# Layer 0 of a two-layer transformer: sums, norms, turns and table entries queued behind the additions out of banks

## The chip, the cores and the metric

The kernel runs on one core of one Trainium2 chip. The metric is the device time of one execution in microseconds (us), the median of three runs. The engines are PE (TensorE: matmuls; PEld is its weight load), DVE (VectorE), ACT (ScalarE), POOL (GpSimd) and SP (SyncE, which here issues most DMAs). Each engine works through its own queue in the order written into the program.

## The reference

The input x has 8 batches of 512 tokens with 512 features. Two layers follow each other, and each is attention, then a feed-forward part, with a residual and a layer norm behind both:

```python
x = layernorm(x + L0_attention(x))   # 16 heads of 32, causal, biases on q, k, v, o
x = layernorm(x + L0_experts(x))     # router picks 2 of 8 experts per token; LoRA on router and experts
x = layernorm(x + L1_attention(x))   # 8 query heads of 64, 2 key/value heads, RMS norm first
x = layernorm(x + L1_ffn(x))         # gate/up/down with integer weights, hidden 1408
```

The change concerns L0 attention, the layer norm behind it, and the router's tables, which are made beside it. In L0 attention `softmax(q k^T / sqrt(32))` is taken without a maximum: exponentials `p`, their row sums, and a division at the end.

## The kernel before, in words

`attention0` holds layer 0's attention for all 8 batches. A batch `b` has 4 groups `g` of 4 heads, and a group has 3 units `u` of key tiles (`UNITS`: key tile 0; key tiles 1 and 3; key tile 2, all causal). So a batch has 12 slots `(g, u)`, written (0,0) to (3,2). In each slot:

- `scores` writes the scores of the unit to four banks (`sc`); ACT takes the exponential (`p`, L1618); POOL cuts the triangle above the diagonal (L1628).
- the thunks of `todo[g, u]` run, then `product` of the unit before (`av`, L1657, and the sum of `p` over key tiles into `total`, L1665 on DVE), then the thunks of `late[g, u]`, and in slots with u = 1 `normalise` of the group before: `ones x total` on PE (`rs`, L1672), an inverse on ACT and DVE (`inverse`, L80 and L81), and `aoT = av * inverse` (L1679).

`plan(b)` fills `todo` and `late` with the work beside the scores: the projections of the batch before (`project`, `ps_o`, added to x at L1532), its layer norm (`env.layernorm`: statistics L217 and L218, the power on POOL at L219 and L220, the norm L222, and a DMA of each tile to `router.rows`), its turn, its router logits (`score`), and the queries, keys and values of the next batch.

Queries and keys of two groups (`queries_and_keys`, a "pair") and the values (`values`) are made by seven products instead of eight, on sums of weight blocks (`seven_of_weights`, L812) and of blocks of xT (`seven_of_rows`, L825). Product n is `ps_{n}of7`; `ORDER` is 1, 6, 2, 5, 3, 7, 4. Product 1 goes out of its bank through ACT (L1502, L1519), the others are added to what is there by DVE: `add` (L1472), product 3 of a pair by L1506; product 7 takes two additions. All these results, `ps_o`, `rs`, the logits and the tables go to two PSUM banks in turn (`Banks`, called `mm`): PE can't begin a result until the one two places before it has been taken out.

The turn of the normed batch for the router is made by DVE in blocks of 32 x 32 (`Turn.blocks`, L125) and through memory: four DMAs out (`turns.out`, L130), one back (`turns.back`, L133), for batches 0 to 5; batches 6 and 7 are turned by PE (`turn`). `load_x(b + 1)` (L1395) is issued behind the return by `behind_return`. `choose` and `dispatch` pick experts on DVE two batches later, `one_hot` (L619, L620) makes 16 one-hot rows on DVE, and `enter` sums them on PE into `ps_table` and adds them to the table (L629 to L631).

The order on PE is the order of the program (`in_order(tc)`). The order on DVE, ACT, POOL and SP is made by the framework's scheduler when the program is built: from its own estimates it takes, of the instructions that are ready, the one that the program has first. `tc.issue_after(ins)` ties every instruction in its block that goes to the engine of `ins` behind `ins` in that order; it adds no wait of its own.

In batch 0 the plan also holds the whole of the queries, keys and values of batch 0 (`query`, `key`, `value`), the sums of weights and `out_of_bias`, which takes the value bias through the output weights (`spread`, L1540, `ps_bias`). In the last batch there is no next batch to prepare. Its slots hold the first rows for the experts (`first_rows`, `first_turned`, `begin`) and the loads of the experts' weights (`experts.load`, L845), which go to the room of the attention weights.

Of the kernel before, what the change touches and what calls it, by code (L numbers as in the profile page):

```python
# [800 lines left out]
def seven_of_weights(nc, w, s, by_rows):  # L801

    def block(i, j):
        if by_rows:
            return w.rearrange("p (g i) f -> p g i f", i=2)[:, :, i, 256 * j : 256 * (j + 1)]
        return w[:, 2 * j : 2 * (j + 1), 256 * i : 256 * (i + 1)]

    def sums():
        for out, a, b, op in ((s[:, 0], block(1, 0), block(1, 1), ALU.add), (s[:, 1], s[:, 0], block(0, 0), ALU.subtract),
                              (s[:, 2], block(0, 1), s[:, 1], ALU.subtract),  # L810
                              (block(1, 0), block(0, 0), block(1, 0), ALU.subtract)):
            nc.vector.tensor_tensor(out, a, b, op)  # L812

    return {1: block(0, 0), 2: block(0, 1), 6: s[:, 1], 5: s[:, 0], 7: block(1, 0), 3: s[:, 2], 4: block(1, 1)}, sums


def seven_of_rows(nc, xT, t):

    def block(i, j):
        return xT[:, 2 * i : 2 * (i + 1), 256 * j : 256 * (j + 1)]  # L820

    def sums():
        for out, a, b in ((t[:, 0], block(0, 1), block(0, 0)), (t[:, 1], block(1, 1), t[:, 0]),
                          (block(0, 1), block(1, 1), block(0, 1)), (t[:, 2], block(1, 0), t[:, 1])):
            nc.vector.tensor_tensor(out, a, b, ALU.subtract)  # L825

    return {1: block(0, 0), 2: block(1, 0), 6: t[:, 1], 5: t[:, 0], 7: block(0, 1), 3: block(1, 1), 4: t[:, 2]}, sums
# [525 lines left out]
def attention0(env, guard, keep, routes, experts, dram, banks, tiles_ctx):  # L1353
# [9 lines left out]
    with ExitStack() as phase:  # L1363
# [61 lines left out]
        ones = own.tile([P, HD], F32, name="ones")  # L1425
        nc.gpsimd.memset(ones, 1.0)

        heads, pairs = {}, {}
        aoTs = {}
        mm = banks  # L1430

# [37 lines left out]
            return ps  # L1469

        def add(out, ps, a):
            nc.vector.tensor_tensor(out, ps, a, ALU.add)  # L1472

        def share(n, ps, block):
            if n == 6:
# [13 lines left out]
        def queries_and_keys(b, pair, n):  # L1489
            if n == 1:  # L1490
                pair_of_heads(b, pair)
            room = pairs[b, pair]
            g = 2 * pair
            ps = seven(n, lambda s, n, k: ((q_of, k_of)[s][n][:, pair, ts(k, P)], x_of[n][:, k, :]))

            def block(i, j):
                return room[:, :, i, 256 * j : 256 * (j + 1)]

            if n == 1:
                for s, at in enumerate((V_BQ, V_BK)):  # L1500
                    for i in (1, 0):
                        nc.scalar.activation(block(i, 0)[:, s, :], ps[:, s, :], AF.Identity,  # L1502
                                             bias=vec[:, at + g + i : at + g + i + 1])
            elif n == 3:
                for s in range(2):
                    nc.vector.scalar_tensor_tensor(block(0, 1)[:, s, :], ps[:, s, :], steps[:, s, pair : pair + 1],  # L1506
                                                   block(1, 1)[:, s, :], ALU.add, ALU.add)
            else:
                share(n, ps, block)
# [18 lines left out]
        def project(b, t, out_of_heads=False):  # L1528
            ps = mm([P, D], "ps_o")
            for c in range(ND):  # L1530
                (wide if out_of_heads else multiply)(ps, aoTs[b][:, c, ts(t, P)], wo[:, c, :], c)
            nc.vector.tensor_tensor(xs[b][:, t, :], ps, xs[b][:, t, :], ALU.add)  # L1532
            if t == NT - 1:
                env.layernorm(b, lambda t: router.rows[router.row_at(b, t) :][:P])

        def out_of_bias():
            ps = mm([P, D], "ps_bias")
            for c in range(ND):
                spread = own.tile([P, P], F32, tag="spread", name="spread", bufs=2)
                nc.vector.tensor_scalar(spread, env.ident, 0.0, bias_v[:, c : c + 1], ALU.mult, ALU.add)  # L1540
                multiply(ps, spread, wo[:, c, :], c)
            nc.vector.tensor_tensor(row[:, 1, :], ps, row[:, 1, :], ALU.add)

        x1Ts, logits = {}, {}
# [8 lines left out]
        def room(b):  # L1553
            x1Ts[b] = work.tile([P, ND, S], F32, tag="x1T", name="x1T")

        def blocks(b):
            room(b)
            flat = x1Ts[b].rearrange("p k s -> p (k s)")
            for t in range(NT):
                turns.blocks(flat, t, xs[b][:, t, :])  # L1560
            turns.out(flat)
            returned[0] = turns.back(flat)

        def turn(b, c, mm=mm):
            if c == 0:
# [81 lines left out]
        def product(b, g, u, p, acc):  # L1647
# [14 lines left out]
            for kt in UNITS[u]:  # L1662
                w = S - P * kt
                if u:
                    nc.vector.tensor_tensor(total[:, :, P * kt :], total[:, :, P * kt :], p[:, :, at : at + w], ALU.add)  # L1665
                at += w

        def normalise(b, g, acc):
# [23 lines left out]
        def plan(b):  # L1692
# [4 lines left out]
            if b == 0:  # L1697
                for slot, thunks in {
                    (0, 0): [lambda: value(0, 0), lambda: value(0, 1)],
                    (0, 1): [lambda: value(0, 3), lambda: query(0, 1)],  # L1700
                    (0, 2): [lambda: value(0, 2), lambda: key(0, 1), lambda: pair_of_heads(0, 1)],
                    (1, 0): [lambda: router.merge_lora(mm([P, ND, E], "ps_wr")), lambda: query(0, 2), lambda: key(0, 2), x_sums],
                    (1, 1): [lambda: query(0, 3), v_sums],
                    (1, 2): [lambda: key(0, 3), q_sums, out_of_bias],
                    (2, 0): [k_sums],
                }.items():
                    todo[slot] += thunks
            if b:
                for t, slot in enumerate(((1, 0), (1, 0), (1, 1), (1, 1)) if last else ((1, 0), (1, 1), (1, 2), (2, 0))):
                    todo[slot].append(lambda t=t: project(pb, t))  # L1710
                for n, (to, *slot) in zip(ORDER, ((todo, 0, 0), (late, 0, 0), (todo, 0, 1), (late, 0, 1), (todo, 0, 2), (late, 0, 2), (todo, 1, 0))):
                    to[tuple(slot)].insert(0, lambda n=n: queries_and_keys(b, 1, n))
            if not last:
                if b:
                    todo[2, 0].append(x_sums)
                for n, (to, *slot) in zip(ORDER, ((todo, 2, 0), (todo, 2, 1), (late, 2, 1), (todo, 2, 2), (late, 2, 2), (todo, 3, 0), (late, 3, 0))):
                    to[tuple(slot)].append(lambda n=n: queries_and_keys(b + 1, 0, n))
                for n, (to, *slot) in zip(ORDER, ((todo, 3, 0), (todo, 3, 1), (todo, 3, 1), (late, 3, 1), (todo, 3, 2), (late, 3, 2), (late, 3, 2))):
# [1 line left out]
            if b > 1:  # L1720
                todo[0, 0].append(lambda: choose(b - 2, mm=aside))
                late[0, 2].append(lambda: dispatch(b - 2))
                todo[1, 2].append(lambda: behind(enter(one_hot(b - 2, range(NT))), normed[0]) if last else enter(one_hot(b - 2, range(NT))))
                if last:
                    todo[1, 2].append(soon)
            if b:
                if by_dma:
                    todo[2, 1].append(lambda: blocks(pb))
                    late[3, 2].append(lambda: score(pb))
                else:  # L1730
                    for c in range(ND):
# [32 lines left out]
        for b in range(NB):  # L1764
            todo, late = plan(b)
            for g in range(ND):
                if b and g == 1 and b + 1 < NB:
                    load_xT(b + 1)
                if g == 3 and b + 1 < NB:
                    with behind_return():  # L1770
                        load_x(b + 1)
                if b == NB // 2 and g == 0:
                    experts.load_lora(work, 1)
                if b == NB - 1:
                    for e in ((0,), (), (1, 2), (3, 4, 7))[g]:
                        experts.load(e)
                acc = []
                for u in range(len(UNITS)):
# [701 lines left out]
```

## Time and profile before

| | us |
|---|---|
| median of 3 runs | 2138.12 (2136.28 to 2138.49) |
| profiled execution, its own time | 2130.51 |
| span of its instructions | 2128.7 |
| PE busy in the span | 2049.1 (96%) |
| DVE busy | 1314.0 (62%) |
| ACT busy | 638.9 (30%) |
| POOL busy | 517.3 (24%) |
| mean granted TensorE clock | 0.996 |

Layer 0's attention takes the first 716 us; from 130 us on a batch takes 83 to 86 us. The experts follow, then layer 1. In rows of the timeline the columns are start and length in us, engine, line, operation, output and inputs by the program's names, shapes and count, and in brackets the idle time before the row and what ended it. `experts` as an operand in layer 0 is the room that the attention weights, xT and the values share with the experts' weights. In rows of waits: who waited for whom, total us, times, longest. A wait is put down to the instruction that came last.

### The profile page before, as it was taken

How to read it: one execution, taken by the hardware profiler on the slowest of the kernel's cores; microseconds unless marked ns; L12 is line 12 of the kernel's file. 1: busy time of each engine (PE TensorE's matmuls, PEld its weight loads, DVE VectorE, ACT ScalarE, POOL GpSimd, SP SyncE). 2: the span in 40 equal slices, each digit the busy share in tenths (PEclk: the TensorE clock that was granted, in tenths of full speed). 3: DMA queues.
4: the chain of work that ended last, by engine and by line, in shares of the span. 5: the costliest groups of instructions: out<-in, count | busy, mean ns of one | idle time of the engine just before them, and what ended most of it. 6: DMA issues, size and time to landing. Idle time of an engine off the chain costs nothing. (4 is left out here: it accounts for less than half of the span.)

```text
span 2128.7 us, 40459 instructions
## 1 busy us (share of the span) xinstructions
PE 2049.1 (96%) x17122; PEld 1117.1 (52%) x17122; DVE 1314.0 (62%) x2155; ACT 638.9 (30%) x930; POOL 517.3 (24%) x509
## 2 busy tenths in 40 slices
PE   8888999999997999999999999999999999999998
PEld 2334444444443677775433333333334888888886
DVE  4657876877867733224236888888857644555443
ACT  2334334343443211111133333333332232222222
POOL 1343534444443311132033312322201000000000
PEclk9999999999999999999999999999999999999999
DMA  6014425235154467887631322232201311111000
GB/s 204 2 57 124 141 80 144 88 103 155 61 176 169 169 169 222 248 243 214 188 113 51 114 75 72 98 119 75 65 1 47 102 60 60 60 60 60 20 20 22
DMA packets 193071, 226.29 MB, mean 106 GB/s; under 512 B 73818, under 2 KB 139610, under 8 KB 189298
## 3 DMA queue, kind: packets, MB, share of 16 engines
q1 hardware_dynamic: 180240, 185.44, 27.8%
q0 software_dynamic: 10560, 34.61, 5.6%
q10 hardware_dynamic: 2082, 3.56, 0.6%
q8 instruction: 138, 2.26, 0.4%
q14 instruction: 51, 0.42, 0.1%
HBM read 138.88 MB, written 84.69 MB: 105 GB/s over the span
## 5 line engine op out<-in xcount | busy, mean ns | idle before, releaser
L1618 ACT ACTIVATE p<-sc 128x2048 f32<-128x2048 f32 (+1 forms) x96 | 152.4, 1587 | 194.6 <-PE sc L67 194.6
L1628 POOL TENSOR_SCALAR_AFFINE_SELECT p<-p 128x512 f32<-128x512 f32 x128 | 98.4, 780 | 383.6 <-ACT p L1618 379.9
L1281 DVE SCALAR_TENSOR_TENSOR hT<-ps_u,vec,sg 128x512 f32<-128x512 f32 x88 | 65.5, 745 | 189.8 <-PE ps_u L1276 189.6
L1292 PE MATMUL ps_f<-ffn_w,h_half 128*128 128x512 f32 x664 | 167.6, 393 | 2.8 <-DVE h_half L1287 2.0
L1009 PE MATMUL ps_gu<-xrT,experts 128*128 128x256 f32 x736 | 166.7, 379 | 0.0
L1009 PEld LDWEIGHTS ps_gu<-xrT,experts 128*128 128x128 f32 x736 | 139.3, 190 | 35.9 <-issue 19.3
L1129 POOL TENSOR_TENSOR g_total<-g_total,r_inv 128x512 f32<-128x512 f32 x64 | 87.7, 1370 | 289.7 <-DVE r_inv L2035 270.6
L2005 ACT ACTIVATE p<-sc 128x1024 f32<-128x1024 f32 x128 | 124.2, 1022 | 100.0 <-PE sc L67 96.5
L1665 DVE TENSOR_TENSOR p<-p 128x1536 f32<-128x1536 f32 (+2 forms) x96 | 147.2, 1533 | 7.9 <-POOL p L1628 2.9
L2035 DVE RECIPROCAL r_inv<-r_inv 128x512 f32<-128x512 f32 x32 | 107.1, 3347 | 71.5 <-ACT r_inv L1126 71.5
L1292 PEld LDWEIGHTS ps_f<-ffn_w,h_half 128*128 128x128 f32 x664 | 122.9, 188 | 34.4 <-DVE h_half L1287 7.4
L1276 PE MATMUL ps_g<-x_high,ffn_w 128*128 128x512 f32 x352 | 137.2, 390 | 0.0
L1276 PE MATMUL ps_g<-x_low,ffn_w 128*128 128x512 f32 x352 | 137.0, 389 | 0.0
L1276 PE MATMUL ps_u<-x_low,ffn_w 128*128 128x512 f32 x352 | 136.9, 389 | 0.0
L1276 PE MATMUL ps_u<-x_high,ffn_w 128*128 128x512 f32 x352 | 136.9, 389 | 0.0
L67 PE MATMUL sc<-qT,kT 64*64 64x512 f32 x1024 | 124.7, 602 | 1.2 <-ACT qT L1899 0.9
L2024 PE MATMUL av<-p,v 128*64 128x512 f32 x512 | 120.8, 593 | 0.0
L1279 ACT ACTIVATE sg<-ps_g,vec 128x512 f32<-128x512 f32 x88 | 60.6, 688 | 195.4 <-PE ps_g L1276 195.4
L67 PE MATMUL ps_o<-attn_out,aoT 128*64 128x512 f32 x512 | 116.4, 598 | 0.0
L67 PE MATMUL ps_q<-hT,attn_qkv 128*64 128x512 f32 (+1 forms) x504 | 116.2, 596 | 0.0
L1126 ACT ACTIVATE r_inv<-rs 128x512 f32<-128x512 f32 x64 | 38.2, 597 | 254.6 <-PE rs L1672 109.2
L219 POOL TENSOR_SCALAR rstd<-mv 128x4 f32<-128x4 f32 x15 | 3.9, 260 | 452.9 <-DVE mv L218 452.9
(317 smaller groups left out, 3584.3 us busy)
## 6 DMA issues: line engine op xcount, KB each, us to landing
results<-y SPq DMA_DIRECT2D x68, 256.0 KB, 2.7
pair<-xrT SPq DMA_DIRECT2D x30, 512.0 KB, 3.1
xrT<-pair SPq DMA_DIRECT2D x120, 128.0 KB, 3.8
turned<-turned SPq DMA_DIRECT2D x56, 256.0 KB, 4.0
merged<-merged SPq DMA_DIRECT2D x48, 256.0 KB, 2.8
experts<-merged SPq DMA_DIRECT2D x8, 1536.0 KB, 8.3
x<-in_x SPq DMA_DIRECT2D x8, 1024.0 KB, 8.7
merged<-in_gate_up SPq DMA_DIRECT2D x32, 256.0 KB, 3.0
```

The source lines that it names most:

```text
L67: nc.tensor.matmul(out[m], lhsT=lhsT[:, m], rhs=rhs, start=start, stop=stop)
L1009: nc.tensor.matmul(ps[:, j, :], lhsT=w, rhs=xT[:, c, :], start=c == 0, stop=c == ND - 1)
L1129: self.nc.gpsimd.tensor_tensor(self.total, self.total, r_inv, ALU.add)
L1276: nc.tensor.matmul(ps, lhsT=w[:, ts(dc, P)], rhs=x[:, dc, :], start=(dc, i) == (0, 0), stop=(dc, i) == (ND - 1, 1))
L1281: nc.vector.scalar_tensor_tensor(hT, u, vec[:, V_SU + c : V_SU + c + 1], sg, ALU.mult, ALU.mult)
L1292: self.nc.tensor.matmul(os[t], lhsT=h[:, ts(t, P)], rhs=self.weights(2 * NHID + c), start=(c, i) == (0, 0), stop=(c, i) == (NHID - 1, 1))
L1618: nc.scalar.activation(p, sc[:, :, :width], AF.Exp, scale=scale)
L1628: select = nc.gpsimd.affine_select(out=first, in_=first, pattern=[[0, 4], [1, P]], compare_op=ALU.is_ge, fill=0.0, base=0, channel_multipl ...
L1665: nc.vector.tensor_tensor(total[:, :, P * kt :], total[:, :, P * kt :], p[:, :, at : at + w], ALU.add)
L2005: nc.scalar.activation(p, sc, AF.Exp, scale=scale)
L2024: nc.tensor.matmul(st["av"][HD * j : HD * (j + 1), :], lhsT=st["v"][:, kt, HD * j : HD * (j + 1)], rhs=p[:, j, :], start=kt == 0, stop=kt ...
L2035: nc.vector.reciprocal(r_inv, r_inv)
```

## The change

Eight things change in `attention0`:

1. `added[0]` keeps the last addition out of a bank that the program has made, and the sums of `p` are tied behind it for all batches but 0.
2. `project` takes the statistics of its tile at once; the norm of the tiles and their DMAs go in two pairs of tiles (`norm_rows`), each tied behind an addition, to (2,0) and (2,1), in the last batch to (1,1) and (1,2).
3. `blocks` goes in two pairs of tiles, tied, to (2,2) and (3,0) instead of whole to (2,1); the load of the next x goes to the end of (3,0).
4. `one_hot` goes in two halves, tied, to (1,0) and (1,1) instead of whole to (1,2).
5. The sums of weights and of xT go in two parts (`sums(False)`, `sums(True)`) and to other slots; in batches 1 to 6 the sums of xT go from (2,0) to (1,2) and (2,0).
6. The four spreads of the bias are made in (1,1), ahead of their products.
7. In the last batch the seven products of the second pair are spread over (0,0) to (2,2) instead of (0,0) to (1,0).
8. Experts 1 and 2 are loaded from group 3 of the last batch on instead of group 2.

```diff
+    def sums(last):   # seven_of_weights; seven_of_rows alike
+        for out, a, b, op in ((block(1, 0), block(0, 0), block(1, 0), ALU.subtract),) if last else (
+                (s[:, 0], block(1, 0), block(1, 1), ALU.add), (s[:, 1], s[:, 0], block(0, 0), ALU.subtract),
+                (s[:, 2], block(0, 1), s[:, 1], ALU.subtract)):
             nc.vector.tensor_tensor(out, a, b, op)
...
         def add(out, ps, a):
-            nc.vector.tensor_tensor(out, ps, a, ALU.add)
+            added[0] = nc.vector.tensor_tensor(out, ps, a, ALU.add)
...
-            nc.vector.tensor_tensor(xs[b][:, t, :], ps, xs[b][:, t, :], ALU.add)
+            add(xs[b][:, t, :], ps, xs[b][:, t, :])
+            if out_of_heads:
+                if t == NT - 1:
+                    env.layernorm(b, lambda t: router.rows[router.row_at(b, t) :][:P])
+                return
+            if t == 0:
+                stats[:] = env.small.tile([P, NT, 6], F32, name="stats"), env.small.tile([P, NT, 2], F32, name="mv")
+            nc.vector.bn_stats(out=stats[0][:, t, :], in_=xs[b][:, t, :])
+            nc.vector.bn_aggr(out=stats[1][:, t, :], in_=stats[0][:, t, :])
             if t == NT - 1:
-                env.layernorm(b, lambda t: router.rows[router.row_at(b, t) :][:P])
+                rstd = env.small.tile([P, NT], F32, name="rstd")
+                nc.gpsimd.tensor_scalar(rstd, stats[1][:, :, 1], LN_EPS, None, ALU.add)
+                nc.gpsimd.tensor_tensor(rstd, rstd, env.neg_half, ALU.pow)
+                stats.append(rstd)
+
+        def norm_rows(b, *tiles):
+            for t in tiles:
+                x = xs[b][:, t, :]
+                nc.vector.tensor_scalar(x, x, stats[1][:, t, 0:1], stats[2][:, t : t + 1], ALU.subtract, ALU.mult)
+                nc.sync.dma_start(out=router.rows[router.row_at(b, t) :][:P], in_=x)
+
+        def behind_add(thunk):
+            with tc.issue_after(added[0].ins):
+                return thunk()
...
-        def blocks(b):
-            room(b)
+        def blocks(b, *tiles):
+            if tiles[0] == 0:
+                room(b)
             flat = x1Ts[b].rearrange("p k s -> p (k s)")
-            for t in range(NT):
+            for t in tiles:
                 turns.blocks(flat, t, xs[b][:, t, :])
-            turns.out(flat)
-            returned[0] = turns.back(flat)
+            if tiles[-1] == NT - 1:
+                turns.out(flat)
+                returned[0] = turns.back(flat)
...
                 if u:
-                    nc.vector.tensor_tensor(total[:, :, P * kt :], total[:, :, P * kt :], p[:, :, at : at + w], ALU.add)
+                    with tc.issue_after(added[0].ins) if b else ExitStack():
+                        nc.vector.tensor_tensor(total[:, :, P * kt :], total[:, :, P * kt :], p[:, :, at : at + w], ALU.add)
...
-                    (0, 1): [lambda: value(0, 3), lambda: query(0, 1)],
-                    (0, 2): [lambda: value(0, 2), lambda: key(0, 1), lambda: pair_of_heads(0, 1)],
-                    (1, 0): [lambda: router.merge_lora(mm([P, ND, E], "ps_wr")), lambda: query(0, 2), lambda: key(0, 2), x_sums],
-                    (1, 1): [lambda: query(0, 3), v_sums],
-                    (1, 2): [lambda: key(0, 3), q_sums, out_of_bias],
-                    (2, 0): [k_sums],
+                    (0, 1): [lambda: value(0, 3), lambda: query(0, 1), lambda: v_sums(False)],
+                    (0, 2): [lambda: value(0, 2), lambda: key(0, 1), lambda: pair_of_heads(0, 1), lambda: q_sums(False)],
+                    (1, 0): [lambda: router.merge_lora(mm([P, ND, E], "ps_wr")), lambda: query(0, 2), lambda: key(0, 2),
+                             lambda: v_sums(True), lambda: k_sums(False)],
+                    (1, 1): [lambda: query(0, 3), lambda: x_sums(False), spread_bias],
+                    (1, 2): [lambda: key(0, 3), out_of_bias, lambda: q_sums(True), lambda: x_sums(True)],
+                    (2, 0): [lambda: k_sums(True)],
...
-                for n, (to, *slot) in zip(ORDER, ((todo, 0, 0), (late, 0, 0), (todo, 0, 1), (late, 0, 1), (todo, 0, 2), (late, 0, 2), (todo, 1, 0))):
+                for n, (to, *slot) in zip(ORDER, (
+                        (todo, 0, 0), (todo, 0, 1), (todo, 0, 2), (todo, 1, 0), (todo, 1, 2), (todo, 2, 1), (todo, 2, 2)) if last else (
+                        (todo, 0, 0), (late, 0, 0), (todo, 0, 1), (late, 0, 1), (todo, 0, 2), (late, 0, 2), (todo, 1, 0))):
                     to[tuple(slot)].insert(0, lambda n=n: queries_and_keys(b, 1, n))
             if not last:
                 if b:
-                    todo[2, 0].append(x_sums)
+                    late[1, 2].append(lambda: x_sums(False))
+                    late[2, 0].append(lambda: x_sums(True))
...
+                rows = []
+                for places, slot in zip(((0, 1), (2, 3)), ((1, 0), (1, 1))):
+                    late[slot].append(lambda places=places: rows.append(behind_add(lambda: one_hot(b - 2, places))))
...
+            if not last:
+                late[3, 0].append(lambda: load_next_x(b + 1))
             if b:
+                for tiles_of, slot in zip(((0, 1), (2, 3)), ((1, 1), (1, 2)) if last else ((2, 0), (2, 1))):
+                    late[slot].append(lambda tiles_of=tiles_of: behind_add(lambda: norm_rows(pb, *tiles_of)))
                 if by_dma:
-                    todo[2, 1].append(lambda: blocks(pb))
+                    late[2, 2].append(lambda: behind_add(lambda: blocks(pb, 0, 1)))
+                    late[3, 0].insert(0, lambda: behind_add(lambda: blocks(pb, 2, 3)))
...
-                    for e in ((0,), (), (1, 2), (3, 4, 7))[g]:
+                    for e in ((0,), (), (), (1, 2, 3, 4, 7))[g]:
```

## The prediction

> **What bounds the kernel now.** I read four views, from coarse to fine. First the busy time of each engine by stage, cut at the borders of the batches of layer 0 (columns: stretch, its length, then busy us and instructions of PE, PEld, DVE, ACT and POOL, the granted clock, the DMA share, GB/s):
>
> ```profile
> 386.00:472.00 86.00, 79.12 (x1365) 37.14 (x1360) 64.67 (x129) 33.54 (x47) 37.97 (x34) 1.00 0.37 112
> 631.00:716.50 85.50, 74.41 (x972) 36.93 (x965) 69.10 (x161) 33.05 (x46) 35.60 (x37) 0.96 0.44 170
> 800.00:2128.00 1328.00, 1314.03 (x6379) 760.50 (x6377) 768.11 (x1079) 357.96 (x551) 211.59 (x213) 1.00 0.32 96
> ```
>
> A middle batch leaves PE idle for 86.0 - 79.1 = 6.9 us, the last one for 11.1. After 800 us PE is idle 1% of the time and starts when layer 0 ends, so what layer 0 saves I carry to the end one for one. DVE, 75% busy in the middle batch, is the only engine that can be late there. Second, what PE waits for from 60 to 735 us (total, times, longest):
>
> ```profile
> PE rs L1672 <- DVE qk L1472: 13.7, 12, 2.1
> PE ps_5of L67 <- DVE qk L1472: 10.2, 7, 4.5
> PE ps_4of L67 <- DVE experts L1472: 9.9, 7, 1.6
> PE ps_3of L67 <- DVE qk L1472: 7.0, 7, 1.4
> PE rs L1672 <- DVE x L1532: 6.0, 5, 3.0
> PE ps_rank L67 <- DVE qk L1506: 3.9, 6, 0.7
> PE sc L67 <- ACT p L1618: 2.0, 2, 1.6
> PE av L1657 <- POOL p L1628: 1.8, 1, 1.8
> ```
>
> With four small rows on DVE (1.6, 1.1, 0.5, 0.4), 54.3 us are waits for DVE. Lines 1472, 1506 and 1532 are the additions out of banks; PE writes two banks in turn, so a late addition stops it. This 54.3 us is the most that better order on DVE can return. Third, what stood before those additions, on DVE in batch 3 (start, us):
>
> ```profile
> 399.48 3.49 DVE L825 TENSOR_TENSOR experts<-experts 128x512 f32<-128x512 f32 x4 [1.96 <-DMA experts<-in_xT]
> ...
> 419.44 1.92 DVE L222 TENSOR_SCALAR x<-x,mv,rstd 128x512 f32<-128x512 f32 x4 [1.48 <-POOL rstd L220]
> 421.27 2.49 DVE L125 STREAM_TRANSPOSE x1T<-x 128x512 f32<-128x512 f32 x4
> 423.68 0.66 DVE L1472 TENSOR_TENSOR qk<-ps_6of,qk 128x512 f32<-128x512 f32 x1
> 424.25 2.54 DVE L1665 TENSOR_TENSOR p<-p 128x1536 f32<-128x1536 f32 x2
> 426.71 0.68 DVE L1472 TENSOR_TENSOR qk<-ps_2of,qk 128x512 f32<-128x512 f32 x1
> ```
>
> and what PE did:
>
> ```profile
> 424.39 1.07 PE L1672 MATMUL rs<-p,ones 128*32 128x512 f32 x8 [1.07 <-DVE qk L1472]
> ...
> 427.44 1.93 PE L67 MATMUL ps_5of<-experts 128*32 128x256 f32 x32 [0.94 <-DVE qk L1472]
> ...
> 455.48 1.04 PE L532 MATMUL ps_logits<-x1T,r_wr 128*32 128x512 f32 x8
> ```
>
> The addition of product 6 stands behind norm and turn, that of product 2 behind a sum of p (1536 and 512 elements, 2.54 us together); rs and product 5 pay. Fourth, the turn's way through memory on the SP queue:
>
> ```profile
> 423.79 3.79 SPq L130 DMA_DIRECT2D turned<-x1T  x4
> 432.41 0.33 SPq L133 DMA_DIRECT2D x1T<-turned  x1
> 432.84 0.39 SPq L1395 DMA_DIRECT2D x<-in_x  x1
> ```
>
> **The change, part by part.** Apart from the reordering, instruction counts stay: the same sums, norms, turns, one-hots and DMAs. So the sum is one of waits removed and waits made, segment by segment of a middle batch.
>
> *Slots (2,u).* Norms now split in two pairs (0.95 us each) behind the additions of project 3 and product 2, turns in two pairs (1.3 us each) behind products 3 and 7, the sum of unit (2,1) behind product 5. Product 6, done at 420.6, is then added at about 421; rs's wait (1.07) and product 5's (0.94) go. What is late next: behind product 3 stand sum, its two steps and a pair of turns, until about 433.7, and product 7's two additions (1.29 us; only 2.2 us of PE work, 1.75 + 0.45, until their bank is wanted) end 0.2 us late. Gain 1.8.
>
> *Slots (3,u).* Wait now: 1.38 at value product 4, behind the sum (3,2) (2.19 us at 450.89). That sum goes behind product 4's addition, where DVE idles 3.37 us: free. But sum (3,1), which ran at 444.4 in idle DVE time, now goes behind value product 3's addition and meets the normalising of the group before (3 x 0.69). Counted from the end of rs: product 3 is ready at 2.8, normalising lasts from 2.0 to 4.1, the addition to 4.8, the sum to 7.3, product 7's additions to 8.6; PE wants that bank for the logits at 7.1. A wait of 1.5 replaces 1.38: gain -0.1.
>
> *Slots (0,u) of the next batch.* Waits now: rs 1.03 (behind the chain of choose, which the change leaves), product 3 0.95 (behind a sum of 2.55), ps_rank 0.65 (behind a sum of 2.18). The last two go; the sum (0,1) then stands before product 7's additions, and product 4 (PE comes to it 1.3 us after 7; two additions last 1.29) waits some 0.7. Gain 0.9.
>
> *Slots (1,u).* Sums of x move from (2,0) to (1,2) and (2,0) and are halved, but nothing ties them to an addition, and the row at 399.48 shows them drawn forward to the load of xT already, so that DVE stood 1.96 us on a DMA. Gain between 0 and the 0.85 of `rs <- DVE x`; I take half, 0.4, because one-hots, now behind additions, leave DVE more room to draw them forward again. The one-hots (16 x 0.22 = 3.5 us) fit under two projections of 3.5 us of PE each.
>
> Middle batch: 1.8 - 0.1 + 0.9 + 0.4 = 3.0. Batches 2 to 6: 15.0. Batch 1 has 3.0 instead of 0.85 at the last point: 3.0 + 1.1 = 4.1.
>
> *Batch 0.* Its sums of p are not tied (b is 0), so the 4.5 at product 5 (behind a sum stretched to 6.95 beside POOL's 6.02 us on x) and 1.6 at product 4 stay. The spreads move ahead of their bank: 1.1 of ps_bias goes. The 12 sums of weights (0.69 to 0.77 us each) leave an early stretch for slots in which DVE idles 3.4 to 6.0 us at a time before additions: 0. Gain 1.1, bounds -3 to +7.
>
> *Last batch.* Seven products of 1.75 us are spread to (2,2), where PE now waits 1.6 on the exponential and 1.8 on POOL; those go, with rs 2.1, product 3 1.4, rank 0.6 and ps_o 0.5: 8.0. Group 3's scores follow product 4 with only 0.9 us of PE between, against 0.85 for its addition, and sums fall beside: -2. Gain 6. Experts 1 and 2 are loaded only after (2,2), about 687, and land 8.3 us each: 696 and 704; expert 1 is first used at 712.2. Free; each further us beyond 16 would be one on PE.
>
> *The turn's return.* Its DMAs issue after the last pair of turns: from 423.8 to about 437.5, or 439.8 if the sum (2,2) and POOL stretch what is before. From the end of the turns to the landing takes 432.41 + 4.9 - 423.76 = 13.6 us, so 451 to 453.5. The logits come at 455.48, less 1.4 if PE stops waiting: 454.1. Covered by 0.6 to 3 us; the longest landings (6.3 and 6.1 against medians of 4.7 and 4.9) would cost some 2. I take 0.3 on each of 6 batches: -1.8. Behind the return on SP stand the load of the next x (432.8 to 449; landed 459 with 9.9; first wanted by POOL at 466.3) and the merging's loads, whose POOL additions have 4 us of idle behind them: 0.
>
> Sum: 15.0 + 4.1 + 1.1 + 6 - 1.8 = 24.4, say 25 us, less than half of the 54.3. The profiled execution took 2130.5 (span 2128.7, 1.8 around it); it should become 2105.5. The median of the runs is 7.6 above that execution, so 2138.1 - 25 = 2113.
>
> A rule weighed here: a sum of 128x1024 took 1.22 us at 409.95 with POOL idle, and 2.18 at 429.50 with POOL adding.
> The Trainium skill's "SBUF — State Buffer", section "SBUF: two separate sides", says that a DVE instruction with two SBUF inputs and a GpSimd one that reads SBUF lock each other out for a whole instruction. That speaks against sums placed beside POOL's work: if each of the 28 tied pairs of sums (1536 and 512) met one more POOL operation of 1.28 us, uncovered, that would be up to 36 us, and no gain would be left. The rows agree that such sums stretch; they do not show that more of them will.
>
> **Rivals.** (a) *All DVE waits go*: the order made at build time places each sum in a gap. For it: DVE idles 21 us in a middle batch. Against: the tight places above. 54.3 less about 8 that nothing touches: 46 plus 3.4 in the last batch, 2089. (b) *Sums collide*: each tied sum delays the next addition. Place: units (g,1), four per batch in seven batches, 28 sums of 2.5 us, before additions with 0.3 to 1.8 us to spare. Uncovered they cost 70, less 46: slower by 24, 2162. It decides from 46 / 28 = 1.6 us per sum. For it: sums reached 4.2 us beside POOL in the last batch. Against: most places spare 1.7 us. (c) *The order hardly moves*: DVE drew the instructions so already, or each wait reappears under another name; 2138.
>
> **How the numbers follow.** Forecast 0.61 (own range 2098 to 2130: gains of 40 to 8), (a) 0.19, (c) 0.06, (b) 0.14. About 0.2%, 4 us, is what a measurement can tell from no change. Faster 0.80, same 0.05 (c and an edge), slower 0.15. The range runs from (a), 2088, to (c), 2138; what it leaves out is (b) and little else.
>
> **What would show it.** Right: `rs <- DVE qk` falls to about 7, product 5 to about 4.5 (batch 0 alone), ps_rank near 0; in (2,u) additions stand before norm, turn and sum. New small waits at product 4 of (1,0) and at ps_logits on DVE, and the SP row of `x1T<-turned` 13 to 16 us later against the batch. Wrong: ps_logits waiting on the return by more than 4 us a batch, rs waiting on a sum of p, or waits on DVE of over 54 us in layer 0.

## The result, and the profile after

The changed kernel takes 2160.65 us (median of 4 runs, 2159.93 to 2162.03), the kernel before beside it 2137.39: a ratio of 1.011, with a 95% interval of 1.0092 to 1.0127. It is slower by 23 us where 25 us of gain were forecast. The profiled executions (2130.5 and 2160.0 us) differ by 29.5: the one of before lies 7 us under its median, the one of after within 1 us. So a difference of spans holds some 6 us that are no part of the change.

Where the time went is read from the start of the router's logits, which ends each batch's preparation. Batch 1's logits start at 195.87 us before and 195.68 after. From there five batches pass up to batch 6's logits: 431.5 us before, 453.8 after. The last batch, from those logits to its output projection, takes 89.2 and then 94.4. The rest differs by 2.2 us. The middle batches hold 22.3 of the 29.6 us by which the spans differ. The busy time by stretch of the kernel before, then of the changed one (columns as in the prediction):

```profile
195.90:627.40 431.50, 398.41 (x6847) 188.49 (x6843) 325.53 (x645) 170.54 (x235) 189.59 (x170) 1.00 0.37 113
```
```profile
195.70:649.50 453.80, 409.29 (x6842) 192.82 (x6843) 338.16 (x646) 170.77 (x235) 194.34 (x170) 0.97 0.35 108
```

Half of the loss in these batches is idle PE (33.1 becomes 44.5 us). The other half is PE itself: the same matmuls take 10.9 us longer, and the granted clock is 0.97 instead of 1.00. What PE waits for in the changed kernel, 60 to 760 us (total, times, longest):

```profile
PE ps_4of L67 <- DVE mine L596: 15.0, 5, 3.1
PE rs L1707 <- DVE qk L1472: 9.3, 5, 2.4
PE ps_logits L532 <- issue: 8.2, 5, 1.6
...
PE ps_2of L67 <- DVE qk L1472: 5.8, 1, 5.8
PE rs L1707 <- DVE p L1700: 4.6, 2, 4.0
```

Old waits are gone (products 3 and 5 in the middle batches, `ps_rank`), and new ones stand at product 4 and longer ones at `rs`. "issue" at `ps_logits` names no releaser; in the DVE rows further below the two additions of value product 7 end just before it (466.76 + 1.28, logits at 468.15). One such batch on PE (start, length, idle time in brackets):

```profile
391.88 1.06 PE L1707 MATMUL rs<-p,ones 128*32 128x512 f32 x8 [2.42 <-DVE qk L1472]
...
394.18 3.31 PE L67 MATMUL ps_3of<-experts 128*32 128x256 f32 x32
...
403.97 3.53 PE L67 MATMUL ps_4of<-experts 128*32 128x256 f32 x32 [2.72 <-DVE mine L596]
...
468.15 1.06 PE L532 MATMUL ps_logits<-x1T,r_wr 128*32 128x512 f32 x8 [1.64 <-issue]
```

The product behind each of the two long waits takes 3.3 to 3.5 us; with no such wait before it, it takes 1.9. The logits, behind 1.64, take their usual time. DVE in batch 1, and then in the batch of the PE rows:

```profile
137.72 4.17 DVE L825 TENSOR_TENSOR experts<-experts 128x512 f32<-128x512 f32 x4 [6.85 <-DMA experts<-in_xT]
...
386.25 1.16 DVE L568 SCALAR_TENSOR_TENSOR rest<-r_hots,pr 128x32 f32<-128x32 f32 x1
...
398.36 4.26 DVE L1700 TENSOR_TENSOR p<-p 128x1536 f32<-128x1536 f32 x2
402.55 1.27 DVE L1472 TENSOR_TENSOR qk<-ps_7of,qk 128x512 f32<-128x512 f32 x2
...
409.12 0.69 DVE L825 TENSOR_TENSOR experts<-experts 128x512 f32<-128x512 f32 x1 [3.71 <-DMA experts<-in_xT]
409.73 0.68 DVE L1472 TENSOR_TENSOR qk<-ps_4of,qk 128x512 f32<-128x512 f32 x1
...
435.67 0.68 DVE L1472 TENSOR_TENSOR qk<-ps_6of,qk 128x512 f32<-128x512 f32 x1
436.47 0.69 DVE L1472 TENSOR_TENSOR qk<-ps_2of,qk 128x512 f32<-128x512 f32 x1
...
442.12 3.81 DVE L1700 TENSOR_TENSOR p<-p 128x1536 f32<-128x1536 f32 x2
445.86 0.86 DVE L1506 SCALAR_TENSOR_TENSOR qk<-ps_3of,steps,qk 128x256 f32<-128x256 f32 x2
...
466.76 1.28 DVE L1472 TENSOR_TENSOR experts<-ps_7of,experts 128x512 f32<-128x512 f32 x2
```

and POOL at the time of `rest` (L568) and of the first of those sums:

```profile
386.08 1.28 POOL L874 TENSOR_TENSOR merged<-merged,scaled 128x512 f32<-128x512 f32 x1 [1.05 <-DMA merged<-in_down]
...
398.07 4.01 POOL L874 TENSOR_TENSOR merged<-merged,scaled 128x512 f32<-128x512 f32 x2
```

Three things are to be seen. The tied sum (0,1), 1536 and 512 elements, takes 4.26 us instead of 2.54, because two additions of POOL (L874, the merging of adapters) run beside it; product 7's additions stand behind it, and product 4 stands behind them. The sum (2,1) takes 3.81 in the same way, and the addition of product 3 stands behind that. And the sums of xT still have no tie: DVE comes to them ahead of an addition and stands on the load of xT, for 3.71 us in the batch of the PE rows, where it was 1.96 before, and for 27.2 us in the five middle batches, where it was 8.5. (The 6.85 us in batch 1 are not new: they were 7.35 before.)

### The profile page after: what moved, and what is told of

Same layout as the page of the kernel before. It is cut to its first block, busy times and chain, and to the rows that moved or that the text cites. A ratio compares the mean times of both kernels' runs of the same rounds, so it can differ in the third digit from the quotient of the medians.

```text
span 2158.3 us, 40427 instructions
## 1 busy us (share of the span) xinstructions
PE 2062.1 (96%) x17122; PEld 1122.0 (52%) x17122; DVE 1325.8 (61%) x2155; ACT 640.0 (30%) x930; POOL 518.6 (24%) x509
## 5 line engine op out<-in xcount | busy, mean ns | idle before, releaser
L1700 DVE TENSOR_TENSOR p<-p 128x1536 f32<-128x1536 f32 (+2 forms) x96 | 154.4, 1608 | 3.5 <-PE av L1691 0.8
L1129 POOL TENSOR_TENSOR g_total<-g_total,r_inv 128x512 f32<-128x512 f32 x64 | 82.7, 1293 | 293.9 <-DVE r_inv L2079 270.3
L1279 ACT ACTIVATE sg<-ps_g,vec 128x512 f32<-128x512 f32 x88 | 60.6, 689 | 195.7 <-PE ps_g L1276 195.7
L67 PE MATMUL ps_o<-experts,aoT 128*32 128x512 f32 x896 | 103.3, 603 | 7.4 <-DVE qk L1472 4.0
```

The costliest lines, as they stand in the source:

```text
L67: nc.tensor.matmul(out[m], lhsT=lhsT[:, m], rhs=rhs, start=start, stop=stop)
L1129: self.nc.gpsimd.tensor_tensor(self.total, self.total, r_inv, ALU.add)
```

## The experiments

All share the changed kernel's code but for the edit shown, except e2 and f4, which are the kernel before with an edit; L1699 is the line that ties the sums of `p`. In the table, "a batch" is a fifth of the time from batch 1's logits to batch 6's, "last" goes from there to the last output projection, and "long" counts PE's waits of 2 us or more between 60 and 760 us. These columns are from the profiled executions, one of each kernel. Beside the experiments the kernel before had medians of 2139.15 to 2139.34 us, and the ratios are to these. Its single executions went from 2129.15 to 2146.02, so a few us between two rows of these columns can be chance.

| kernel | us, ratio to before (95%) | first logits | a batch | last | PE busy | long |
|---|---|---|---|---|---|---|
| before | 2137.39 | 195.9 | 86.30 | 89.2 | 2049.1 | 3 |
| changed | 2160.65, 1.011 (1.0092 to 1.0127) | 195.7 | 90.76 | 94.4 | 2062.1 | 12 |
| e1 sums of p untied | 2156.25, 1.0085 (1.0052 to 1.0119) | 192.3 | 90.06 | 94.0 | 2054.5 | 10 |
| e2 before + sums of p tied | 2182.37, 1.0202 (1.0174 to 1.0231) | 202.6 | 95.31 | 90.1 | 2068.3 | 25 |
| e3 turn in one piece | 2176.86, 1.0187 (1.016 to 1.0215) | 198.1 | 92.68 | 92.6 | 2065.9 | 18 |
| e4 last batch as before | 2161.1, 1.0102 (1.0075 to 1.0129) | 196.3 | 91.17 | 94.0 | 2061.8 | 15 |
| f1 sums of p untied, of xT tied | 2128.09, 0.9942 (0.9924 to 0.996) | 188.4 | 86.08 | 96.1 | 2052.7 | 4 |
| f2 sums of xT tied | 2149.14, 1.0043 (1.0029 to 1.0056) | 193.3 | 90.23 | 93.9 | 2060.4 | 11 |
| f4 before + sums of xT tied | 2139.34, 1.0004 (0.9987 to 1.002) | 195.0 | 87.84 | 89.2 | 2057.1 | 8 |
| f5 no merging additions | 2125.47, 0.9933 (0.9912 to 0.9955) | 187.5 | 85.64 | 91.2 | 2049.8 | 8 |
| g1 f1 + last batch as before | 2126.58, 0.9934 (0.9912 to 0.9957) | 188.9 | 85.95 | 92.5 | 2047.0 | 4 |
| g2 g1 + sums (g,2) tied | 2125.91, 0.9921 (0.9892 to 0.995) | 188.4 | 85.75 | 94.3 | 2053.5 | 6 |
| h1 f2 + POOL's additions later | 2135.82, 0.9986 (0.9969 to 1.0003) | 188.9 | 87.67 | 93.2 | 2053.4 | 10 |
| h2 g2 + POOL's additions later | 2141.89, 1.0007 (0.9991 to 1.0024) | 189.9 | 88.19 | 94.2 | 2061.3 | 15 |

**First round: which part of the change costs.** e1 takes the tie off the sums of `p`:

```diff
-                    with tc.issue_after(added[0].ins) if b else ExitStack():
+                    with ExitStack():
```

> The changed kernel, but no sum of p is tied behind an addition; all else stays. Theory S (the tied sums of units (g,1) meet POOL's work, hold up product 7's additions, and PE's waits of about 3 us then slow its clock): of the changed kernel's waits per middle batch, product 4 on DVE (3.0 and 1.6 of slowed PE behind it), product 1 (1.0) and ps_logits (1.6) go, 7.2 x 6 = 43 us; the waits at products 5, 3, ps_rank and value product 4 of the kernel before come back, 3.8 x 6 = 23. Net 20 faster than the changed kernel: 2135 to 2145 us, and the mean granted clock back at 0.994 or more. Theory R (the later return of the turn moves the merging's loads and POOL's additions beside the chain of choose, and that is the loss): 2155 us or more, rs still waits 2.2 in slots (0,1).

It came back by only 4 us. Theory S is missed by 11; the time lies in the band of theory R, but `rs` waits 1.3 us on average there, not 2.2. Product 4's wait on `mine` went, and another took its place on PE (the timeline of e1):

```profile
403.58 5.34 PE L67 MATMUL ps_o<-experts,aoT 128*32 128x512 f32 x32 [2.23 <-DVE qk L1472]
```

With the sums of `p` free again DVE is done earlier, takes the first sum of xT earlier (402.24), and stands 6.28 us on its load instead of 3.71; the additions come behind it. The waits at `ps_o` grow from 7.5 us in all to 22.4. Each cost hides the other, so neither can be measured by removing one alone.

e2 is the kernel before with nothing but this tie:

```diff
+            added[0] = nc.vector.tensor_tensor(out, ps, a, ALU.add)
...
+                    with tc.issue_after(added[0].ins) if b else ExitStack():
                         nc.vector.tensor_tensor(total[:, :, P * kt :], total[:, :, P * kt :], p[:, :, at : at + w], ALU.add)
```

> The kernel before, with the sums of p of batches 1 to 7 tied behind the last addition out of a bank, and nothing else of the change. Theory S: the whole loss is here, 2155 to 2165 us, with the wait of about 3 us at product 4 and a granted clock below 0.99. Theory R: without the later return the ties only help, 2115 to 2130 us (the 3.8 us per batch of waits behind sums go).

It is 43 us slower than the kernel before beside it, 17 above the band of theory S: `rs` waits 29.9 us on additions and 12.8 on sums of `p`, product 4 18.1, `ps_logits` 15.1. Tied alone, the sums are the worst of all these kernels; the rest of the change makes up about half of it.

e3 turns the batch in one piece behind an addition of (2,1) and loads the next x as early as before:

```diff
-                    late[2, 2].append(lambda: behind_add(lambda: blocks(pb, 0, 1)))
-                    late[3, 0].insert(0, lambda: behind_add(lambda: blocks(pb, 2, 3)))
+                    late[2, 1].append(lambda: behind_add(lambda: blocks(pb, 0, 1, 2, 3)))
```

> The changed kernel, but the turn stands whole at the end of (2,1), tied behind the addition of product 2, and the next x is loaded at the start of group 3, as before; so the return on SP and the merging's loads behind it come some 13 us earlier again. Theory R: rs in slots (0,1) waits 1.0 instead of 2.2, and without that and what follows of it 2145 us or less. Theory S: only this 1.2 x 5 = 6 us, partly given back because the turn now stands before product 5's addition: 2154 to 2160 us, product 4 still waits 3 us.

`rs` fell to 1.0 us a batch, as the theory of the return has it, but the whole turn in one place made `ps_1of` wait about 2.0 and `ps_logits` 2.5 a batch, and the time rose to 2176.86, above the bands of both theories. The return is a small cause, and the split of the turn is worth having.

e4 puts the last batch back: its seven products in (0,0) to (1,0), and experts 1 and 2 loaded from group 2 on:

```diff
-                        (todo, 0, 0), (todo, 0, 1), (todo, 0, 2), (todo, 1, 0), (todo, 1, 2), (todo, 2, 1), (todo, 2, 2)) if last else (
...
-                    for e in ((0,), (), (), (1, 2, 3, 4, 7))[g]:
+                    for e in ((0,), (), (1, 2), (3, 4, 7))[g]:
```

> The changed kernel, but in the last batch the seven products of the second pair and the loads of experts 1 and 2 stand where they stood before. From the first wait of the last batch to the end the changed kernel takes 7.5 us more than the kernel before. Theory L (the spreading is a loss of its own: product 2 waits 5.8 us behind choose, ps_x1T 3.2 behind the norm): 2150 to 2155 us. Theory S (the spreading gains what the prediction said, 6 us, and the 5.8 and 3.2 come from ties): 2160 to 2168 us.

There is no difference from the changed kernel, so neither the loss of theory L nor the gain of theory S; a wait of 3.9 at `rs` replaced one of 5.8 at `ps_2of`.

**Second round: the sums of xT, and POOL.** f2 ties the sums of xT as the other work is tied, and f1 does that with the sums of `p` untied:

```diff
-                    late[1, 2].append(lambda: x_sums(False))
-                    late[2, 0].append(lambda: x_sums(True))
+                    late[1, 2].append(lambda: behind_add(lambda: x_sums(False)))
+                    late[2, 0].append(lambda: behind_add(lambda: x_sums(True)))
```

> The changed kernel with its sums of x in (1,2) and (2,0) tied behind additions too; its sums of p stay tied. Theory X: the waits of ps_o on DVE (7.5 us) and about 4 us of slowed PE go: 2146 to 2153 us; product 4 of queries still waits 3 us a batch. Theory not-X: 2158 us or more.

> The changed kernel, with its sums of p not tied and its sums of x, in (1,2) and (2,0), tied behind additions. Theory X (with the one-hots tied away, the order made at build time draws the sums of x ahead of product 4's addition, where DVE stands 4 to 6 us on the load of xT and PE waits behind it, its clock halved): the waits of ps_o on DVE, 22.4 us in the kernel with untied sums alone, fall to under 4, with some 8 us of slowed PE: 2120 to 2132 us, faster than the kernel before. Theory not-X (these waits come from the one-hots or the statistics): 2145 us or more.

f2 returns 11.5 us; the waits at `ps_o` go from 7.5 us to 1.4. f1 returns 32.6, to 11 below the kernel before beside it; both times lie in the bands of theory X. Untying the sums of `p` is worth 4 us while the sums of xT are free and 21 once they are tied. The waits of f1:

```profile
PE ps_5of L67 <- DVE qk L1472: 12.3, 8, 4.5
PE ps_4of L67 <- DVE experts L1472: 9.9, 7, 1.6
PE rs L1707 <- DVE qk L1472: 6.5, 5, 1.9
```

The first two are rows of the kernel before at about their old size. `rs` waits 6.5 us instead of 13.7, and no longer for the addition to x (6.0 before), but `ps_o` waits 4.7 for that. A batch takes 86.08 us, against 86.30. What f1 gains in this profile lies ahead of batch 1's logits, 7.5 us: the waits of 3.0 at `rs` for the addition to x, of 1.1 at `ps_bias` and of 1.1 at `rs` are gone there, and PE is busy for 2.6 us less. The last batch takes 6.9 of it back, so the two spans (2128.7 and 2127.5) differ by 1.2 only; the profiled execution of the kernel before lies 7 us under its median. Where the rest of the 11 us between the medians lies, no profile here shows.

f4 gives the kernel before the split and tied sums of xT alone:

```diff
-                    todo[2, 0].append(x_sums)
+                    late[1, 2].append(lambda: behind_add(lambda: x_sums(False)))
+                    late[2, 0].append(lambda: behind_add(lambda: x_sums(True)))
```

> The kernel before, with nothing of the change but the split of the sums of x over (1,2) and (2,0), tied there behind additions. Theory X: the waits of rs on the addition of ps_o, 6.0 us, go, little else: 2130 to 2135 us. Otherwise 2138 us within 2.

Nothing is won: the 6.0 us of `rs <- DVE x` go, and `rs <- DVE qk` rises from 13.7 to 25.2. There the norms and the whole turn come next on DVE; what the sums no longer hold up, these do.

f5 keeps every tie of the changed kernel and leaves out POOL's merging additions, so the experts' weights lack their adapters:

```diff
-        return {0: load, 1 + i: lambda: nc.gpsimd.tensor_tensor(w[0], w[0], scaled, ALU.add),
+        return {0: load, 1 + i: lambda: None,
```

> The changed kernel without the merging's additions on POOL (line 874; the experts' adapters are left out of their weights, their DMAs stay). Theory S-port (sums of p of 1536 and 512 take 3.6 to 4.3 us instead of 2.5 because they run beside POOL's two additions): those sums fall to 2.5 to 3 us, product 4 waits 1.3 to 1.8 instead of 3.0 and the slowed products behind it go: 2140 to 2148 us. If the place of the sums alone is the cause, whatever POOL does: 2156 us or more.

It is 35 us faster than the changed kernel, twice what was expected, though product 4 still waits 2.2 us and not 1.3 to 1.8. The waits that answer to the first two rows of the changed kernel:

```profile
PE ps_4of L67 <- DVE mine L596: 11.2, 5, 2.2
...
PE rs L1707 <- DVE qk L1472: 5.1, 5, 1.0
```

The sum (0,1) takes 2.73 us there. What still holds product 4 is the normalising of the group before (L80, L81, L1714): product 3 ends at 376.73, but its addition stands behind `aoT` and starts at 377.87, with the sum and product 7's additions behind it. Besides the sums, small instructions of DVE get shorter. The chain of `choose` from its first row (L551) to the addition behind it takes 9.30 us in the changed kernel (381.84 to 391.14) and 7.90 here (364.11 to 372.01), as it did before. In it `rest` (L568) takes 1.16 us while POOL adds, 0.19 otherwise. That is most of the chain's growth, and the chain's growth of 1.40 is that of the wait at `rs`, 1.03 to 2.42.

f5 does more than free these instructions, though. The load of xT stands on SP behind a DMA that waits for POOL's addition (in the changed kernel 402.11, the addition ending at 402.08, the load at 403.08); without the additions it is issued 20.0 to 23.4 us after the logits instead of 24.6 to 26.3, and DVE stands on it for 15.0 us in the middle batches instead of 27.2. Also, 8 of the 35 us lie ahead of batch 1's logits, where the changed kernel had lost nothing, and no run takes the additions out of the kernel before. So the 35 us are what these additions cost by all ways together, not their part in the loss; h1 below is the closer test of that.

**Third round: can the additions live beside each other?** g1 is f1 with e4's edit; g2 ties the sums of units (g,2) alone:

```diff
+                    with tc.issue_after(added[0].ins) if b and u == 2 else ExitStack():
```

> The changed kernel with sums of p untied and sums of xT tied, and the last batch put back as before: its seven products spread over (0,0) to (1,0), experts 1 and 2 loaded from group 2 on. Theory L: the spread products and late loads of the last batch cost the 7.4 us that this batch still takes more than in the kernel before; then 2119 to 2124 us, and 1501 to 1503 us from the last batch's logits to the end. Rival: the last batch loses for other reasons (the split norms and one-hots, half clock); then about 2128 and 1506 to 1509.

> As the kernel above, with the sums of units (g,2) tied behind additions and those of units (g,1) free. Theory T: what hurts in the ties is the sums of units (g,1), 1536 elements that come to stand beside POOL's merging additions; the sums of units (g,2) find idle DVE time behind product 4. Then the waits of 1.38 and 0.65 a batch go and the time is 2106 to 2116 us. Rival: any tie of a sum moves a late addition elsewhere; then 2124 or more.

g1's last batch is 3.6 us shorter than f1's, but the two totals can't be told apart (the runs of f1 are 2127.23 to 2130.52, of g1 2125.84 to 2128.47): theory L had 4 to 9. Three more us of that batch against before remain unexplained. g2 misses its mark: the sums of 1024 do fall to 1.2 us each, from 2.1, and the waits for `experts` at product 4 go, but `rs` (14.4 us) and `av <- POOL p` (7.7) take what they gave. A late addition moved elsewhere, as the rival said, though at no loss against g1.

h1 is f2, all ties in place, with POOL's merging additions queued behind the cut of the triangle of their slot:

```diff
-            with behind_return() if g == 3 and u else ExitStack():
+            with behind_return() if g == 3 and u else ExitStack(), tc.issue_after(select.ins):
```

> The changed kernel with sums of xT tied and its tied sums of p, and POOL's merging additions queued behind the cut of the triangle of their slot; nothing is left out. Theory P: product 4's 15 us of waits come from sums that are stretched beside those additions; moved, the sums of unit (0,1) take 2.5 to 3 us instead of 4.26, product 4 waits 1.8 us or less, 2130 to 2140 us. Rival: DVE has no room for the tied sums even unstretched, or the additions meet other sums there; then 2148 or more, as with sums of xT tied alone.

> The second of these kernels (sums of (g,2) tied, last batch as before) with POOL's merging additions queued behind the cut as well. If both theories hold, 2104 to 2114 us, 0 to 4 below the second kernel; if POOL's additions only matter where tied sums of (g,1) meet them, no difference from the second kernel (within 2 us).

h1 lands in the band of its theory, 13 us below f2, with nothing left out of the computation. The sum (0,1) of the batch shown takes 2.54 us again instead of 4.26:

```profile
385.65 2.54 DVE L1700 TENSOR_TENSOR p<-p 128x1536 f32<-128x1536 f32 x2
```

The waits of h1:

```profile
PE rs L1707 <- DVE qk L1472: 19.7, 11, 3.1
...
PE ps_4of L67 <- DVE mine L596: 7.5, 5, 2.3
```

Product 4's wait is halved, to a mean of 1.5: 1.0 in three batches, and 2.25 in two, above the bound named. The additions now run beside `choose` and beside the stretch ahead of `rs`, which pays 3.2 us more than in f2. h2 applies the same edit to g2 and loses 16 us: there the untied sums (2,1) and (3,1) stand early, and in the same batch they now take 3.90 and 3.65 us (3.02 and 2.56 in g2) beside the moved additions. Which order of POOL is good depends on where DVE's sums stand; neither theory for h2 had a loss in it.

The best of these kernels, f1, g1 and g2, take 2126 to 2128 us and beat both kernels by 0.6 to 0.8% of the time before and 1.5 to 1.6% of the time after. They can't be ranked among themselves.

## Why the prediction was wrong, point by point

**The step that failed is slots (0,u).** The prediction had 0.9 of gain a batch there. Products 3 and the rank did lose their waits, as it said. But product 4, priced at 0.7, waited 2.7 to 3.1. Two things were missing from that price. The sum ahead of product 7's additions was counted near its undisturbed 2.5 us and took 4.26 in the batch shown and 3.61 in the next. And the normalising of the group before, counted in slots (3,u) but not here, can stand ahead of product 3's addition: with sums of 2.5 to 2.7 us product 4 waits 1.0 in three batches of h1, where product 3 itself is late, and 2.2 in the other two and in all of f5. `rs`, said to stay at 1.03, went to 2.42. PE then ran slowly for a product after each, 1.4 and 1.6 us more. In the batch shown that is 1.6 us of old waits won against 1.4 + 2.7 + 1.4 + 1.6 = 7.1 lost: 5.5 on the wrong side, more than the whole 4.46 that a batch grew by.

**The rule on the shared port was weighed and then left out of the sum.** The prediction quoted the Trainium skill's "SBUF — State Buffer", section "SBUF: two separate sides", and held that the rows "do not show that more of them will" stretch. In the middle batches of the changed kernel they do: the mean sum of 1536 takes 2.25 us, against 1.75 before, and that of 512 takes 1.38, against 0.69. The sums of 1024 fall from 1.94 to 1.31 at the same time, so the ties also exchanged which sums meet POOL; what costs is that the stretched ones now stand ahead of additions. One of the two rows that the prediction read for this was misread: POOL wasn't idle beside the sum at 409.95. Its addition of `g_total` began 0.24 us later and took 2.12 us instead of 1.28; at 429.50 it began 0.18 us earlier and the sum took 2.18 instead of 1.22. In these two rows the instruction that starts second is the one that gets longer. Rival (b), slower at 2162, named sums that delay the next addition, and its time is within 2 us of the result. That nearness is luck: the sums did not cost their whole length at 28 places, and part of the loss comes from the sums of xT. They cost at (0,1) and (2,1), by waiting and, at (0,1), by the slow matmuls behind.

**Slots (1,u) failed too.** The prediction gave 0.4 for sums of xT "drawn forward again". They were drawn forward further: DVE stands 3.6 to 7.2 us a batch on the load, against 1.3 to 2.0 before. In batch 1, where it stood 7 us in both kernels, the wait of 3.0 at `rs` did not shrink but became 4.0, now on the sum of `p` that is tied behind. f2 puts the price at 11.5 us in all. The reason given, that the one-hots leave DVE more room, had the sign wrong: as e1 shows, a DVE that is done earlier only comes to the waiting instruction earlier (6.28 us on the load instead of 3.71).

**Right, or nearly.** In (2,u) the additions of products 6 and 2 are at 435.67 and 436.47, ahead of sum and turn, and `rs` and product 5 wait for nothing; but the sum of 3.81 makes value product 1 wait 1.0 on product 3's addition, so the gain was 1.0, not 1.8. At `ps_logits` 1.6 replaced 1.38, as said (1.5). The first product 5, in batch 0, kept its 4.5. The return of the turn was covered, and came 14.0 us later against the batch, within the 13 to 16 named (issued at 459.10, before at 432.41). What it carried along was not free, though. The merging's loads stand behind it on SP, so their additions on POOL moved into `choose`. The prediction had written 0 for them, looking only at POOL's own idle time; e3 (return early) and f5 (no additions) both bring `rs` back to 1.0.

**The last batch** was to gain 6 and lost 5.2. Product 6 now comes one slot later ((0,1) instead of (0,0)), and its addition on DVE stands behind the whole chain of `choose` (653.83 to 664.51) where it stood inside the chain before; product 2 waits 5.8 for it. f1 shows the same with 4.1. Undoing the spread returns 3.6 where the sums are free (g1), and nothing where they are tied (e4). Of what batches 0 and 1 were to win ahead of batch 1's logits, 0.2 came.

**The sum itself left out a cost.** Every wait was priced at its length. In the profiles here PE's busy time rises with the number of long waits, from 2049.1 us with 3 to 2068.3 with 25: 19.2 / 22 = 0.9 us for each, an estimate from single executions. In its middle batches, with 8 such waits against none, the changed kernel pays 10.9 us in this way. That the 4.46 us a batch are made of these parts is read from rows; that the ties and the free sums of xT cause them is shown by f1 and f2, and the place of POOL's additions by h1 (13 us below f2, nothing left out). Of the prediction's own signs of being wrong, two came: `rs` waits on a sum of `p`, and the waits on DVE listed for the changed kernel's layer 0 add up to more than 54 us (61.6, without those named "issue"). Not settled are how the loss divides between POOL's additions, the normalising and the chain of `choose`, 3 us of the last batch, and 2 us behind layer 0's attention, where profiled executions of these kernels differ by up to 5.6 us.

**And the hoped gain was not there to win.** With the sums of xT tied and the ties of `p` taken off in full or in part, f1's middle batches are 0.2 us shorter than before and g2's 0.6, not 3.0, measured against an execution of the kernel before that lies 7 us under its median. In f1 most of the old waits stand where they stood, and `ps_o` waits where `rs` waited; in g2 DVE's queue was rearranged, and the freed waits came back at other banks. Rival (c) described the middle batches better than the forecast did.

## What to carry to other kernels

Before a piece of work is pinned behind another on one engine, look at what the other engine of a shared port does at the new place, price the work at its stretched length, and list everything that already stands ahead of it there. If most of a family of instructions is tied, tie the one that waits on a load as well, or it becomes the head of the queue. And undo parts in pairs: here one tie hid the other, and single undoings showed 4 and 11 us of a joint 33.

## What the runs showed of the hardware that was not expected

A long wait of PE often costs more than its length, but not every time. In the changed kernel the next product ran slowly behind waits of 2.42 to 3.12 us (3.3 to 3.6 us instead of 1.9), and in e1 an output projection behind 2.06 and 2.23 (5.3 instead of 3.6); the mean granted clock of the middle batches is 0.97. Behind 2.92 in the changed kernel nothing slowed, and in e2 the same wait of 3.12 us at product 4 slowed it in one batch and not in four others. Counted in the rows of all fourteen profiles from 60 to 760 us, PE's instructions in the 6 us behind a wait took over 0.5 us more than usual after 4 of 132 waits of 1.3 to 1.8 us, 32 of 79 of 2 to 3, 25 of 33 of 3.0 to 3.6, and all 37 above that. The Trainium skill's "TensorE: Matmul & The Clock Gate", section "Part 1: The HAM clock gate", gives half clock after an idle window of about 3.4 us, in windows that run freely. The halved speed agrees, and it fits windows that run freely that one and the same wait slows PE or doesn't. The length doesn't agree as a limit: waits of 2.06 us were enough at times, and the measurement decides. That the clock is the cause is an inference from the lengths and the granted clock; no run here held the clock apart from the waits.

What stretches the sums also reaches instructions of hardly any size: 128 x 32 elements of DVE took 1.16 us instead of 0.19 beside one POOL addition of 1.28 (the rows at 386.25 and 386.08). In that batch the chain of `choose`, made of such instructions, grew by 1.4 us and the long sum (0,1) by 1.7; each is paid by the addition behind it.
